# Edge weights made in PSUM in every layer, and one-hot matrices made tile by tile

## The chip, the cores and the metric

The kernel runs on one core of a Trainium2 chip. The metric is the time of one execution on the device in microseconds, as the median of three runs.

## The reference

A graph network of three layers over 6250 nodes and 100,000 edges, 256 features wide. Edges are sorted by destination, and the destinations are denser at low node numbers.

```python
ew = edge_attr @ edge_w + edge_b                      # [100000, 32] @ [32, 256]
rel_masks = [(edge_type == i) for i in range(3)]
inv_cnt = [1 / max(segment_sum(m, dst), 1) for m in rel_masks]
for l in range(3):
    residual = x
    msg = relu(x[src] * ew)
    out = 0
    for i in range(3):
        h = segment_sum(msg * rel_masks[i][:, None], dst) * inv_cnt[i][:, None]
        out = out + h @ weights[l, i]
    out = out + x @ roots[l] + biases[l]
    x = residual + relu(out)
return layernorm(x0 + x)                              # x0: the input x
```

The edge weights `ew` do not depend on the layer.

## The kernel before

Edges are taken in 782 tiles of 128, and two tiles make a pair; there are 391 pairs. A layer is one loop over steps `it`. Each step handles several pairs at different stages of one software pipeline, and the program's order within a step is each engine's order, since the schedule is written out by hand. `order` lists the pairs: from number 60 upward to the last, then from 59 down to 0. `pair(k)` is the pair that is k steps ahead.

For each pair of tiles:

- `gather` (L575, POOL's queue) fetches the source rows `x[src]` by two indirect DMAs, one for each tile, into `xs`, a tile with 16 buffers. It runs `AHEAD` = 8 steps ahead.
- `weigh` (L612, VectorE) multiplies `xs` by the edge weights, three steps ahead; `bound` (L615, ScalarE) applies the relu.
- `one_hot` (L619, VectorE) makes, for both tiles by one instruction, a matrix of 128 edges by 120 columns (three relations by 40 node places) that is one where the column equals the edge's number in `seg`.
- `reduce` (L629, TensorE) multiplies messages by one-hots, which sums the messages of the 40 nodes for each relation, into `h_p` in PSUM.
- `add` (L645, VectorE) adds `h_p` to the accumulator `acc` in SBUF, `LAG` steps later (1 in the first layer, 3 in the later ones).

In the first layer the edge weights are made as well. The raw attributes of eight tiles are loaded by one DMA (`load_attrs`), transposed on TensorE two pairs at a time (`turn`, L589, into `turn_p`), copied to SBUF by ScalarE (`keep_attrs`, L595, into `at`), multiplied by `edge_w` on TensorE (`make_ew`, L602, into `ew_p` in PSUM) and copied to SBUF by ScalarE (`keep_ew`, L609, into `ew_s`). Bias and product come in one matmul through a row of ones. From `ew_s`, four pairs at a time, 1 MB is stored to `ew_all` in DRAM (`store_ew`, SP's queue). The later layers load it back, 1 MB for four pairs (`load_ew`, L552, SP's queue).

Beside the edges run the nodes, 49 blocks of 128. `root_turn`, `root_turned`, `root_mul` and `root_keep` (L650 to L661) make x times `roots` and the bias. When the last edge of a block has been added, `node_mul` (L673, TensorE) multiplies the sums by `weights`, `node_end` (L700 to L707, VectorE) scales them, adds the root part, applies the relu and stores the block to `x_mid` in DRAM, and `clear` (L690, ScalarE) empties its place in `acc`. The steps at which blocks end come from `schedule`; they lie closer together as node numbers rise, because later nodes have fewer edges. The next layer's gathers read `x_mid`, so the first of them waits for its last store. In the last layer a layer norm follows each block (L710 to L721).

[...]

Of the kernel before, what the change touches and what calls it, by code (L numbers as in the profile page):

```python
# [442 lines left out]
def ordered_path(ctx, tc, x, edge_attr, weights, roots, biases, edge_w, edge_b, out, src_i, seg, place_i, consts):  # L443
# [13 lines left out]
    A1 = A + 1  # L457
    DC = D // P
    UP = P // 2
    AR = UP + A1  # L460
    WK = R * WIN
    AHEAD = 8
    order, _, moved, least, most = schedule(N, E, 1)
    reach = []
    for u, (lo, hi) in enumerate(zip(least, most)):
# [47 lines left out]
    groups = list(dict.fromkeys(u // 4 for u in order))  # L513

    def first_of(p, n):
        return p == 0 or order[p - 1] // n != order[p] // n

    def last_of(p, n):
        return p == U - 1 or order[p + 1] // n != order[p] // n
# [25 lines left out]
        nc.sync.dma_start(b_sb, biases[l:l + 1, :].to_broadcast([P, D]))  # L545
        return r_sb, b_sb

    def load_ew(l, g):
        ew = edge.tile([P, 4, 2, D], F32, name="ew_s", bufs=3)
        if l > 0:  # L550
            n = min(4, U - 4 * g)
            nc.sync.dma_start(ew[:, :n].rearrange("p k i d -> p (k i d)"), ew_all[g, :, :n * 2 * D])  # L552
        return ew

    def layer(l, r_sb, b_sb, ews, pools):
        h_pool = pools.enter_context(tc.tile_pool(name="h_p", bufs=2 if l == 0 else 5, space=PSUM))
        if l == 0:
            ew_pool = pools.enter_context(tc.tile_pool(name="ew_p", bufs=1, space=PSUM))
# [8 lines left out]
        xs, ew_ps, ats, ohs, h_ps, turns, o_ps, rs = {}, {}, {}, {}, {}, {}, {}, {}  # L567
        x0s, mvs, oh_bs, t_ss, places = {}, {}, {}, {}, []
        r_next, ews_next = (None, None), {}

        def gather(u):
            xs[u] = edge.tile([P, 2, D], F32, name="xs", bufs=16)
# [6 lines left out]
        def store_ew(g):  # L579
            n = min(4, U - 4 * g)  # L580
            nc.sync.dma_start(ew_all[g, :, :n * 2 * D], ews[g][:, :n].rearrange("p k i d -> p (k i d)"))

        def pairs_of(q):
            return range(min(2, U - 2 * q))
# [6 lines left out]

        def keep_attrs(q):
            n = len(pairs_of(q))
            ats[q] = edge.tile([AR, 2, P], F32, name="at", bufs=1)
            nc.scalar.activation(ats[q][:, :n], turns[q][:AR, :n, :], AF.Copy)  # L595

        def make_ew(q):

            ew_ps[q] = ew_pool.tile([P, 2, 2, D], F32, name="ew_p")
            for k in pairs_of(q):  # L600
                for i in range(2):
                    nc.tensor.matmul(ew_ps[q][:, i, k, :], ats[q][i * UP:i * UP + A1, k, :],  # L602
                                     ew_sb[i * UP:i * UP + A1, :], start=True, stop=True)

        def keep_ew(q):
            if q // 2 not in ews:
                ews[q // 2] = load_ew(0, q // 2)
            for k in pairs_of(q):
                nc.scalar.activation(ews[q // 2][:, q % 2 * 2 + k], ew_ps[q][:, :, k, :], AF.Copy)  # L609

        def weigh(u):
            nc.vector.tensor_mul(xs[u], ews[u // 4][:, u % 4], xs[u])  # L612

        def bound(u):
            nc.scalar.activation(xs[u], xs[u], AF.Relu)  # L615

        def one_hot(u):
            ohs[u] = edge.tile([P, 2, WK], F32, name="oh", bufs=6)
            nc.vector.tensor_tensor(ohs[u], iota_w[:, None, :].to_broadcast([P, 2, WK]),  # L619
                                    seg[:, 2 * u:2 * u + 2, None].to_broadcast([P, 2, WK]), op=ALU.is_equal)  # L620
# [120 lines left out]
        for it in range(-9, max(starts) + 6):  # L741
            def pair(k):
                return order[it + k] if 0 <= it + k < U else None
            if pair(AHEAD) is not None:
                gather(pair(AHEAD))
            if l == 0 and pair(9) is not None and first_of(it + 9, 4):
                load_attrs(pair(9) // 4)
            if l > 0 and pair(AHEAD) is not None and pair(AHEAD) // 4 not in ews:
                ews[pair(AHEAD) // 4] = load_ew(l, pair(AHEAD) // 4)
            if l == 0 and it >= -4 and (it + 4) % 20 == 0 and (it + 4) // 20 * 6 < NT - 1:  # L750
                load_x((it + 4) // 20 * 6)
            if it == 10:
                nc.sync.dma_start(w_sb, weights[l].rearrange("r (c p) e -> p (r c) e", p=P))
            if l == L - 1 and it + 2 in root_at:
                load_x0(root_at[it + 2])
            if l < L - 1 and it == U - 10:
                r_next = load_root(l + 1)
            if l < L - 1 and U <= it < U + 2:
                ews_next[groups[it - U]] = load_ew(l + 1, groups[it - U])
# [40 lines left out]
        return (*r_next, ews_next)  # L800

    with tc.manual_schedule():
        state = (*load_root(0), {})
# [4 lines left out]

WIN = 40
RING = 1024
ASIDE = RING + WIN
ROOTS = 16
PACK = 2048


def schedule(N, E, lag):

    P = 128
    U = -(-E // (2 * P))
    NT = -(-N // P)
    done = []
    for c in range(NT):
        edges = E * min(1.0, (P * (c + 1) / N) ** 0.5)
        done.append(U if c == NT - 1 else min(U, -(-int(edges) // (2 * P)) + 4))  # L830
    K = -(-done[0] // 4) * 4
# [12 lines left out]
    least = [node(2 * P * u - 1024) for u in range(U)]  # L844
    most = [node(2 * P * u + 1024) for u in range(U)]


    for p, u in enumerate(order, lag):
        if u >= K:
            assert all(p <= starts[c] or least[u] >= P * (c + 1) for c in range(2, NT))  # L850
            assert p <= moved or least[u] >= 2 * P
            assert all(p < starts[c] or least[u] >= P * c for c in range(8, NT, 8))
            for b in range(RING // P + 1, (most[u] + WIN - 1) // P + 1):
                assert (moved + 2 if b - RING // P == 1 else starts[b - RING // P] + 3) < p
        else:
            assert most[u] <= 2 * P and (p <= starts[1] or most[u] + WIN <= P)
    return order, starts, moved, least, most
# [149 lines left out]
```

## Time and profile before

| | |
|---|---|
| three runs | 3131.9, 3129.4, 3127.8 us; median 3129.4 |
| profiled execution | 3133.5 us, its span 3131.7 us |
| granted TensorE clock, mean | 0.855 |
| busy, share of the span | PE 78%, PE weight loads 67%, VectorE 64%, ScalarE 42%, POOL 75% |
| DMA | 668 MB, mean 213 GB/s; SP's and ScalarE's queues 32.2% of the engines, POOL's 31.6% |
| largest issues on SP | 194 loads of `ew_s` and 97 stores to `ew_all`, 1 MB each |
| gathers | 782 in the first layer, 1564 in the later two |

The busy share of an engine is the union of its instructions over the span. A group's line gives the program line, the engine, the operation, the tiles it writes and reads, shapes and count, then busy time and the mean of one instruction in nanoseconds, then the idle time in front of it and what ended that. A source line's answer gives the shortest, median and longest duration, and the starts of the first and last instruction. In the timeline each row begins with start and duration in microseconds. In a table by window the columns are length, PE, PE's weight loads, VectorE, ScalarE and POOL busy, then the clock, the DMA share and GB/s.

### The profile page before, as it was taken

How to read it: one execution, taken by the hardware profiler on the slowest of the kernel's cores; microseconds unless marked ns; L12 is line 12 of the kernel's file. 1: busy time of each engine (PE TensorE's matmuls, PEld its weight loads, DVE VectorE, ACT ScalarE, POOL GpSimd, SP SyncE). 2: the span in 40 equal slices, each digit the busy share in tenths (PEclk: the TensorE clock that was granted, in tenths of full speed). 3: DMA queues.
4: the chain of work that ended last, by engine and by line, in shares of the span. 5: the costliest groups of instructions: out<-in, count | busy, mean ns of one | idle time of the engine just before them, and what ended most of it. 6: DMA issues, size and time to landing. Idle time of an engine off the chain costs nothing.

```text
span 3131.7 us, 50860 instructions
## 1 busy us (share of the span) xinstructions
PE 2429.6 (78%) x14938; PEld 2108.6 (67%) x14938; DVE 2003.2 (64%) x4664; ACT 1302.0 (42%) x2524; POOL 2354.9 (75%) x3118
## 2 busy tenths in 40 slices
PE   4898999999998766677777777767677777877765
PEld 3777777778887666666666666656566666666665
DVE  4566666777776455566666666645566677777765
ACT  3666666666776422222333333222223333333332
POOL 7777777777777677777777777767777777777775
PEclk9899899999998778778888888766887888888886
DMA  4777776766776665656666666656666666666664
GB/s 135 233 233 231 222 241 213 228 216 217 230 231 213 217 218 199 213 200 218 205 217 205 221 221 217 206 184 223 211 208 223 220 217 209 224 228 216 218 216 138
DMA packets 295322, 668.14 MB, mean 213 GB/s; under 512 B 147224, under 2 KB 181996, under 8 KB 257788
## 3 DMA queue, kind: packets, MB, share of 16 engines
q1 hardware_dynamic: 175832, 350.27, 32.2%
q0 software_dynamic: 112608, 307.65, 31.6%
q10 hardware_dynamic: 6596, 6.87, 0.6%
q8 instruction: 124, 2.03, 0.3%
q14 instruction: 162, 1.33, 0.1%
HBM read 542.90 MB, written 121.70 MB: 212 GB/s over the span
## 4 chain that ended last, share of the span: by engine, by line
PE 31%; DMA 21%; issue 19%; POOL 17%; DVE 9%; ACT 2%; DVEq 1%; POOLq 0%; ACTq 0%
POOL xs L575 16%; PE h_p L629 15%; DMA xs<-x_mid,src_io 15%; PE o_p L673 7%; DMA xs<-in_x_dram,src_io 6%; PE ew_p L602 4%; DVE x_root L704 3%; DVE xs L612 2%; PE r_p L658 2%; DVE acc L645 2%; PE turn_p L589 1%; ACT ew_s L609 1%; POOL limits L926 1%; DVEq L645 1%; DVE oh L619 1%
## 5 line engine op out<-in xcount | busy, mean ns | idle before, releaser
L575 POOL DMA_INDIRECT xs<-x_mid,src_io x1564 | 1537.5, 983 | 509.0 <-issue 404.6
L629 PE MATMUL h_p<-oh,xs 128*128 128x120 f32 x9384 | 1451.6, 311 | 445.0 <-issue 177.8
L629 PEld LDWEIGHTS h_p<-oh,xs 128*128 128x128 f32 x9384 | 1364.3, 223 | 541.6 <-issue 309.4
L612 DVE TENSOR_TENSOR xs<-ew_s,xs 128x512 f32<-128x512 f32 x1173 | 808.0, 689 | 913.5 <-DMA xs<-x_mid,src_io 566.8
L615 ACT ACTIVATE xs<-xs 128x512 f32<-128x512 f32 x1173 | 739.5, 630 | 1484.9 <-DVE xs L612 1466.3
L575 POOL DMA_INDIRECT xs<-in_x_dram,src_io x782 | 789.6, 1010 | 247.1 <-issue 158.7
L645 DVE TENSOR_TENSOR acc<-h_p,acc 128x240 f32 (+1 forms) x1173 | 519.5, 443 | 147.0 <-PE h_p L629 74.7
L673 PE MATMUL o_p<-w_sb,acc 128*128 128x256 f32 (+1 forms) x1764 | 503.5, 428 | 89.2 <-DVE acc L645 52.1
L619 DVE TENSOR_TENSOR oh<-iota_w,seg_o 128x240 f32<-128x240 f32 x1173 | 467.0, 398 | 0.0
L673 PEld LDWEIGHTS o_p<-w_sb,acc 128*128 128x128 f32 (+1 forms) x1764 | 361.7, 216 | 152.4 <-DVE acc L645 57.6
L658 PE MATMUL r_p<-r_sb,t_s 128*128 128x256 f32 x588 | 216.3, 504 | 79.5 <-ACT t_s L654 78.8
L602 PE MATMUL ew_p<-ew_sb,at 33*128 33x256 f32 x1564 | 235.2, 421 | 10.9 <-ACT at L595 8.8
L609 ACT ACTIVATE ew_s<-ew_p 128x512 f32<-128x512 f32 x391 | 209.4, 587 | 41.5 <-PE ew_p L602 40.5
L704 DVE SCALAR_TENSOR_TENSOR x_root<-o_p,inv,x_root 128x256 f32<-128x256 f32 (+1 forms) x441 | 212.4, 482 | 20.9 <-PE o_p L673 8.6
L623 ACT ACTIVATE oh_b<-oh 128x240 bf16<-128x240 f32 x391 | 160.0, 409 | 117.9 <-DVE oh L619 111.0
L658 PEld LDWEIGHTS r_p<-r_sb,t_s 128*128 128x128 f32 x588 | 130.0, 245 | 111.3 <-ACT t_s L654 95.5
L602 PEld LDWEIGHTS ew_p<-ew_sb,at 33*128 33x128 f32 x1564 | 141.7, 195 | 44.8 <-ACT at L595 16.3
L690 ACT ACTIVATE acc<-zero_o 128x768 f32<-128x768 f32 (+1 forms) x150 | 141.0, 940 | 15.8 <-PE o_p L673 9.2
L629 PE MATMUL h_p<-oh_b,full_ones 128*128 128x120 bf16 x782 | 109.3, 223 | 0.0
L589 PE MATMUL turn_p<-ident_o,an 128*128 128x128 f32 x391 | 89.4, 312 | 7.9 <-DMA an<-in_edge_attr_dram 7.8
L589 PEld LDWEIGHTS turn_p<-ident_o,an 128*128 128x128 f32 x391 | 40.7, 145 | 77.1 <-issue 75.9
L650 PE MATMUL r_p<-ident_o,x_all 128*128 128x128 f32 x294 | 64.1, 303 | 30.9 <-DVE x_root L661 24.8
(84 smaller groups left out, 609.0 us busy)
## 6 DMA issues: line engine op xcount, KB each, us to landing
ew_s<-ew_all SPq DMA_DIRECT2D x194, 1024.0 KB
ew_all<-ew_s SPq DMA_DIRECT2D x97, 1024.0 KB
xs<-x_mid,src_io POOLq DMA_INDIRECT x1564
xs<-in_x_dram,src_io POOLq DMA_INDIRECT x782
an<-in_edge_attr_dram SPq DMA_DIRECT2D x97, 128.0 KB
x_mid<-x_all SPq DMA_DIRECT2D x96, 128.0 KB
x_all<-in_x_dram ACTq DMA_DIRECT2D x8, 768.0 KB
x<-in_x_dram SPq DMA_DIRECT2D x48, 128.0 KB
```

The lines of the kernel that those rows point to most:

```text
L575: nc.gpsimd.indirect_dma_start(out=xs[u][:, i, :], out_offset=None, in_=x_rows[:, :], in_offset=bass.IndirectOffsetOnAxis(ap=src_i[:, t:t ...
L589: nc.tensor.transpose(turns[q][:, k, :], ans[groups.index(q // 2) % 3][:, q % 2 * 2 + k].rearrange("p i a -> p (i a)"), ident)
L602: nc.tensor.matmul(ew_ps[q][:, i, k, :], ats[q][i * UP:i * UP + A1, k, :], ew_sb[i * UP:i * UP + A1, :], start=True, stop=True)
L609: nc.scalar.activation(ews[q // 2][:, q % 2 * 2 + k], ew_ps[q][:, :, k, :], AF.Copy)
L612: nc.vector.tensor_mul(xs[u], ews[u // 4][:, u % 4], xs[u])
L615: nc.scalar.activation(xs[u], xs[u], AF.Relu)
L619: nc.vector.tensor_tensor(ohs[u], iota_w[:, None, :].to_broadcast([P, 2, WK]), seg[:, 2 * u:2 * u + 2, None].to_broadcast([P, 2, WK]), op= ...
L629: nc.tensor.matmul(h_ps[u][:, d, :], xs[u][:, i, d * P:(d + 1) * P] if d < DC else full_ones, (ohs if d < DC else oh_bs)[u][:, i, :], star ...
L645: nc.vector.tensor_tensor(there, h_ps[u][:, :CH].rearrange("p c (r w) -> p c r w", r=R), there, op=ALU.add)
L658: nc.tensor.matmul(rs[c][:, 1, :], t_ss[c][:, d, :], r_sb[:, d, :], start=(d == 0), stop=(d == DC - 1))
L673: nc.tensor.matmul(o_p[:n, r, :], acc[:, d, r, slot:slot + n], w_sb[:, r * DC + d, :], start=(d == 0), stop=(d == DC - 1))
L704: nc.vector.scalar_tensor_tensor(root, o_p[:n, r, :], inv[:n, c, r:r + 1], root, op0=ALU.mult, op1=ALU.add)
```

## The change

The edge weights are no longer stored. The first layer keeps the transposed attributes instead, eight pairs (`GROUP`) in one tile `at` of 128 rows, and stores these to `at_all` in DRAM, 512 KB for eight pairs. The later layers load `at`, and every layer runs `make_ew` for two pairs at once. `weigh` takes the edge weights from `ew_p` in PSUM, so ScalarE's copy `keep_ew` and the tile `ew_s` are gone. A step that opens a new group of two pairs makes their weights first and weighs both pairs; the step after weighs none. `add` now stands ahead of `weigh` in a step. `h_p` has three buffers in the later layers, where `ew_p` takes two banks. `LAG` is 2 there, `AHEAD` is 9 in all, and the pairs turn around at 64.

`one_hot` uses two instructions, one for each tile, each with the tile's column of `seg` as a scalar for each partition.

```diff
-    AHEAD = 8
+    AHEAD = 9
...
-    ew_all = dram.tile([(U + 3) // 4, P, 8 * D], F32, name="ew_all")
+    at_all = dram.tile([(U + GROUP - 1) // GROUP, P, GROUP * P], F32, name="at_all")
...
-    def load_ew(l, g):
-        ew = edge.tile([P, 4, 2, D], F32, name="ew_s", bufs=3)
+    def pairs_in(g):
+        return min(GROUP, U - GROUP * g)
+
+    def load_at(l, g):
+        at = edge.tile([P, GROUP, P], F32, name="at", bufs=3)
         if l > 0:
...
+            nc.sync.dma_start(at[:, :pairs_in(g)].rearrange("p k e -> p (k e)"), at_all[g, :, :pairs_in(g) * P])
+        return at
...
-        h_pool = pools.enter_context(tc.tile_pool(name="h_p", bufs=2 if l == 0 else 5, space=PSUM))
+        h_pool = pools.enter_context(tc.tile_pool(name="h_p", bufs=2 if l == 0 else 3, space=PSUM))
+        ew_pool = pools.enter_context(tc.tile_pool(name="ew_p", bufs=1, space=PSUM))
...
-        LAG = 1 if l == 0 else 3
+        LAG = 1 if l == 0 else 2
...
         def keep_attrs(q):
             n = len(pairs_of(q))
-            ats[q] = edge.tile([AR, 2, P], F32, name="at", bufs=1)
-            nc.scalar.activation(ats[q][:, :n], turns[q][:AR, :n, :], AF.Copy)
+            g = 2 * q // GROUP
+            if g not in ats:
+                ats[g] = load_at(0, g)
+            nc.scalar.activation(ats[g][:, 2 * q % GROUP:2 * q % GROUP + n], turns[q][:, :n, :], AF.Copy)
...
-        def keep_ew(q):
-            if q // 2 not in ews:
-                ews[q // 2] = load_ew(0, q // 2)
-            for k in pairs_of(q):
-                nc.scalar.activation(ews[q // 2][:, q % 2 * 2 + k], ew_ps[q][:, :, k, :], AF.Copy)
-
         def weigh(u):
-            nc.vector.tensor_mul(xs[u], ews[u // 4][:, u % 4], xs[u])
+            nc.vector.tensor_mul(xs[u], ew_ps[u // 2][:, :, u % 2, :], xs[u])
...
         def one_hot(u):
             ohs[u] = edge.tile([P, 2, WK], F32, name="oh", bufs=6)
-            nc.vector.tensor_tensor(ohs[u], iota_w[:, None, :].to_broadcast([P, 2, WK]),
-                                    seg[:, 2 * u:2 * u + 2, None].to_broadcast([P, 2, WK]), op=ALU.is_equal)
+            for i in range(2):
+                nc.vector.tensor_scalar(ohs[u][:, i, :], iota_w, seg[:, 2 * u + i:2 * u + i + 1], None,
+                                        op0=ALU.is_equal)
...
+            two = [order[p] for p in range(it + 3, min(it + 5, U)) if order[p] // 2 == pair(3) // 2] if (
+                pair(3) is not None and first_of(it + 3, 2)) else []
+            if two:
+                make_ew(two[0] // 2)
             if pair(0) is not None:
                 reduce(pair(0))
-            if pair(3) is not None:
-                weigh(pair(3))
-                bound(pair(3))
             if pair(-LAG) is not None:
                 add(pair(-LAG))
+            for u in two:
+                weigh(u)
+                bound(u)
             if l == 0:
 
-                for k, work in ((4, keep_ew), (5, make_ew), (6, keep_attrs), (7, turn)):
+                for k, work in ((5, keep_attrs), (6, turn)):
                     if pair(k) is not None and first_of(it + k, 2):
                         work(pair(k) // 2)
-                if pair(3) is not None and last_of(it + 3, 4):
-                    store_ew(pair(3) // 4)
+                if pair(3) is not None and last_of(it + 3, GROUP):
+                    store_at(pair(3) // GROUP)
...
-    K = -(-done[0] // 4) * 4
+    K = -(-done[0] // GROUP) * GROUP
```

More of the change, by code (lines that the diff above doesn't have):

```diff
@@ L459, in ordered_path @@
     UP = P // 2
-    AR = UP + A1
     WK = R * WIN
-    AHEAD = 8
+    AHEAD = 9
     order, _, moved, least, most = schedule(N, E, 1)
@@ L513, in ordered_path @@
     groups = list(dict.fromkeys(u // 4 for u in order))
+    at_groups = list(dict.fromkeys(u // GROUP for u in order))
     def first_of(p, n):
@@ L546, in load_root, with layer @@
         return r_sb, b_sb
-    def load_ew(l, g):
-        ew = edge.tile([P, 4, 2, D], F32, name="ew_s", bufs=3)
+    def pairs_in(g):
+        return min(GROUP, U - GROUP * g)
+    def load_at(l, g):
+        at = edge.tile([P, GROUP, P], F32, name="at", bufs=3)
         if l > 0:
[L551 to L555, printed above, removed]
-        h_pool = pools.enter_context(tc.tile_pool(name="h_p", bufs=2 if l == 0 else 5, space=PSUM))
+            nc.sync.dma_start(at[:, :pairs_in(g)].rearrange("p k e -> p (k e)"), at_all[g, :, :pairs_in(g) * P])
+        return at
+    def layer(l, r_sb, b_sb, ats, pools):
+        h_pool = pools.enter_context(tc.tile_pool(name="h_p", bufs=2 if l == 0 else 3, space=PSUM))
+        ew_pool = pools.enter_context(tc.tile_pool(name="ew_p", bufs=1, space=PSUM))
         if l == 0:
-            ew_pool = pools.enter_context(tc.tile_pool(name="ew_p", bufs=1, space=PSUM))
             t_pool = pools.enter_context(tc.tile_pool(name="turn_p", bufs=1, space=PSUM))
-        LAG = 1 if l == 0 else 3
+        LAG = 1 if l == 0 else 2
         starts = schedule(N, E, LAG)[1]
@@ L566, in layer @@
         CH = DC + 1 if l == 0 else DC
-        xs, ew_ps, ats, ohs, h_ps, turns, o_ps, rs = {}, {}, {}, {}, {}, {}, {}, {}
+        xs, ew_ps, ohs, h_ps, turns, o_ps, rs = {}, {}, {}, {}, {}, {}, {}
         x0s, mvs, oh_bs, t_ss, places = {}, {}, {}, {}, []
-        r_next, ews_next = (None, None), {}
+        r_next, ats_next = (None, None), {}
         def gather(u):
@@ L577, in gather, with store_at @@
                     in_offset=bass.IndirectOffsetOnAxis(ap=src_i[:, t:t + 1], axis=0))
-        def store_ew(g):
-            n = min(4, U - 4 * g)
-            nc.sync.dma_start(ew_all[g, :, :n * 2 * D], ews[g][:, :n].rearrange("p k i d -> p (k i d)"))
+        def store_at(g):
+            nc.sync.dma_start(at_all[g, :, :pairs_in(g) * P], ats[g][:, :pairs_in(g)].rearrange("p k e -> p (k e)"))
         def pairs_of(q):
@@ L601, in make_ew @@
                 for i in range(2):
-                    nc.tensor.matmul(ew_ps[q][:, i, k, :], ats[q][i * UP:i * UP + A1, k, :],
+                    nc.tensor.matmul(ew_ps[q][:, i, k, :],
+                                     ats[2 * q // GROUP][i * UP:i * UP + A1, (2 * q + k) % GROUP, :],
                                      ew_sb[i * UP:i * UP + A1, :], start=True, stop=True)
-        def keep_ew(q):
-            if q // 2 not in ews:
-                ews[q // 2] = load_ew(0, q // 2)
-            for k in pairs_of(q):
-                nc.scalar.activation(ews[q // 2][:, q % 2 * 2 + k], ew_ps[q][:, :, k, :], AF.Copy)
         def weigh(u):
-            nc.vector.tensor_mul(xs[u], ews[u // 4][:, u % 4], xs[u])
+            nc.vector.tensor_mul(xs[u], ew_ps[u // 2][:, :, u % 2, :], xs[u])
         def bound(u):
@@ L747, in layer @@
                 load_attrs(pair(9) // 4)
-            if l > 0 and pair(AHEAD) is not None and pair(AHEAD) // 4 not in ews:
-                ews[pair(AHEAD) // 4] = load_ew(l, pair(AHEAD) // 4)
+            if l > 0 and pair(AHEAD) is not None and pair(AHEAD) // GROUP not in ats:
+                ats[pair(AHEAD) // GROUP] = load_at(l, pair(AHEAD) // GROUP)
             if l == 0 and it >= -4 and (it + 4) % 20 == 0 and (it + 4) // 20 * 6 < NT - 1:
@@ L758, in layer @@
             if l < L - 1 and U <= it < U + 2:
-                ews_next[groups[it - U]] = load_ew(l + 1, groups[it - U])
+                ats_next[at_groups[it - U]] = load_at(l + 1, at_groups[it - U])
+            two = [order[p] for p in range(it + 3, min(it + 5, U)) if order[p] // 2 == pair(3) // 2] if (
+                pair(3) is not None and first_of(it + 3, 2)) else []
+            if two:
+                make_ew(two[0] // 2)
             if pair(0) is not None:
                 reduce(pair(0))
-            if pair(3) is not None:
-                weigh(pair(3))
-                bound(pair(3))
             if pair(-LAG) is not None:
                 add(pair(-LAG))
+            for u in two:
+                weigh(u)
+                bound(u)
             if l == 0:
-                for k, work in ((4, keep_ew), (5, make_ew), (6, keep_attrs), (7, turn)):
+                for k, work in ((5, keep_attrs), (6, turn)):
                     if pair(k) is not None and first_of(it + k, 2):
                         work(pair(k) // 2)
-                if pair(3) is not None and last_of(it + 3, 4):
-                    store_ew(pair(3) // 4)
+                if pair(3) is not None and last_of(it + 3, GROUP):
+                    store_at(pair(3) // GROUP)
             if it in root_at:
@@ L799, in layer @@
                 one_hot(pair(3))
-        return (*r_next, ews_next)
+        return (*r_next, ats_next)
     with tc.manual_schedule():
@@ L814 @@
 ROOTS = 16
+GROUP = 8
 PACK = 2048
```

## The prediction

> **What bounds the kernel now.** I read the engine table first: PE has the largest busy share, which need not make it the bound. Then the costliest groups, then the gathers' own line.
>
> ```profile
> PE 2429.6 (78%) x14938; PEld 2108.6 (67%) x14938; DVE 2003.2 (64%) x4664; ACT 1302.0 (42%) x2524; POOL 2354.9 (75%) x3118
> ...
> L575 POOL DMA_INDIRECT xs<-x_mid,src_io x1564 | 1537.5, 983 | 509.0 <-issue 404.6
> L612 DVE TENSOR_TENSOR xs<-ew_s,xs 128x512 f32<-128x512 f32 x1173 | 808.0, 689 | 913.5 <-DMA xs<-x_mid,src_io 566.8
> L575 POOL DMA_INDIRECT xs<-in_x_dram,src_io x782 | 789.6, 1010 | 247.1 <-issue 158.7
> L619 DVE TENSOR_TENSOR oh<-iota_w,seg_o 128x240 f32<-128x240 f32 x1173 | 467.0, 398 | 0.0
> ```
> ```profile
> L575 POOL DMA_INDIRECT xs<-x_mid,src_io x1564: 942/946/1456, 1082.1 to 3111.4; - x196
> L575 POOL DMA_INDIRECT xs<-in_x_dram,src_io x782: 942/946/1627, 38.3 to 1064.9; - x196
> ...
>   DMA x_mid<-x_all: 32.8, 2
> ```
>
> POOL issues 2346 gathers back to back from 38.3 to 3112.3 us. In 3074 us it is busy 1537.5 + 789.6 = 2327.1; the other 747 are a constant 0.30 us between two gathers (2343 x 0.305 = 714) and two waits at the layer changes (32.8). It never waits for a buffer, so in steady state nothing else sets the pace. The span is 38.3 start + 2346 x 0.946 = 2219 + lengthened gathers 108 + 747 between + 19.4 tail = 3131.7.
>
> The 108 us: the median gather takes 946 ns, the means are 983 and 1010, so 1564 x 0.037 + 782 x 0.064 = 108. The timeline shows where they come from.
>
> ```profile
> 1608.44 0.94 POOL L575 DMA_INDIRECT xs<-x_mid,src_io  x1 [0.30 <-DMA xs<-x_mid,src_io]
> 1609.57 0.69 DVE L612 TENSOR_TENSOR xs<-ew_s,xs 128x512 f32<-128x512 f32 x1 [1.61 <-DMA xs<-x_mid,src_io]
> 1609.69 1.39 POOL L575 DMA_INDIRECT xs<-x_mid,src_io  x1 [0.30 <-issue]
> ...
> 1611.05 0.68 DVE L612 TENSOR_TENSOR xs<-ew_s,xs 128x512 f32<-128x512 f32 x1
> 1611.38 1.17 POOL L575 DMA_INDIRECT xs<-x_mid,src_io  x1 [0.30 <-issue]
> ...
> 1613.54 1.51 DVE L704 SCALAR_TENSOR_TENSOR x_root<-o_p,inv,x_root 128x256 f32<-128x256 f32 x3
> ...
> 1614.42 0.95 POOL L575 DMA_INDIRECT xs<-x_mid,src_io  x1 [0.30 <-issue]
> ```
>
> A gather that starts while `weigh` (L612, both inputs in SBUF) runs lasts 0.946 plus what is left of the `weigh`, less 0.127: 1609.69 starts with 0.57 left and takes 1.39. One that starts under L704, whose first input is PSUM, takes 0.95. I sorted all gathers of the trace by the DVE instruction running at their start: under L612 480, lengthened by 82.4 us in all; under L619 (one-hots, both inputs SBUF) 349 by 22.6; under other instructions with two SBUF inputs 3; under none (873), or one with a PSUM input (L645 355, L704 161, L661 41), zero.
>
> **The change, part by part.** The sum is made against the profiled execution (span 3131.7, time 3133.5; the median of the three runs is 4.1 below).
>
> `weigh` from PSUM: its second input leaves SBUF, so the 82.4 go. Its own time stays 0.69: L661 (PSUM and SBUF) has 414 ns, L663 (both SBUF) 415 at the same 128x256.
>
> One-hots: the tensor_tensor of 398 ns becomes two tensor_scalars of 120 elements with a scalar column. The 22.6 of the old form go. The nearest row is L719.
>
> ```profile
> L719 DVE TENSOR_SCALAR x_all<-x_all,mv x49: 411/423/572, 2244.8 to 3125.4; 128x256 f32<-128x256 f32 x48, 106x256 f32<-106x256 f32 x1
> ```
> Taking off 136 elements at 1.07 ns (the slope from L619 to L612) gives 0.27 us; at half that slope 0.34. I take 0.27. Successive DVE instructions start about 0.08 before the former's end, so a pair's one-hots cost 0.38 of DVE instead of 0.32: 70 us more over 1173 pairs, up to 235 at 0.34. DVE is 64% busy and trails POOL, so this alone is free.
>
> [...] Fourteen gathers start under L719: none is lengthened. But L719 itself grows: eighteen that start with 0.3 to 0.4 us of a gather left average 505 ns. [...] I take 5, keep 0 to 25.
>
> Edge weights on PE: layers 2 and 3 gain 391 x 4 matmuls with their weight loads. In layer 1's timeline eight records (one group of two pairs) go from 700.58 to the next PE group at 701.65: 1.07, so 0.535 per pair, 209 us per layer. Those layers keep PE busy 66 to 78% of each 200 us window at a granted clock of 0.72 to 0.89, so there is room. In layer 1 nothing is added, but PE has no room.
>
> ```profile
> 660.00:860.00 200.00, 192.62 (x1430) 161.69 (x1429) 146.49 (x335) 139.15 (x295) 153.68 (x153) 1.00 0.70 222
> 1660.00:1860.00 200.00, 155.45 (x909) 138.36 (x908) 133.83 (x314) 65.09 (x109) 152.56 (x156) 0.89 0.64 212
> ```
> First column after the length is PE: 192.6 of 200 at full clock in layer 1, 155.5 in layer 2. In layer 1's stretch of close node blocks (17 in 70 pairs by the schedule) PE needs, from starts in the timeline, 70 x (0.99 reduce + 0.535 weights + 0.14 turns) + 17 x 2.96 node products + 12 x 1.09 root products = 180 us; POOL without lengthening passes those pairs in 70 x 2.50 = 175. So half of layer 1 (460 to 960) cannot speed up: 25 of its 50 us stay.
>
> New waits there: `ew_p` is one buffer, freed by DVE's second `weigh` instead of ACT's copy, and that `weigh` waits for its gather. Behind it on DVE stand the one-hots and the next `add`; `reduce` on PE waits for both (`h_p` has two buffers in layer 1, three later instead of five). With 16 gather buffers POOL can run about 10 pairs, 25 us, beyond today's lag (reduce starts 11 to 18 us after the gather in layer 1), which absorbs most. `add` now stands ahead of the `weigh`s in the step, so it no longer waits for a gather with them; the order's turning point moves from pair 60 to 64, which shifts node blocks by 4 steps and costs nothing. No row shows the loop; its bounds are 0 and, if every pair of layer 1 paid 0.2 us beyond POOL's pace, 80. I take 10.
>
> Layer changes: the drain now includes weights on PE; LAG falls by one. I add 2 each, 4.
>
> Removed: 194 loads and 97 stores of 1 MB on SP's queue (some 307 of 668 MB) and 391 ACT copies (209 us). No gather waits for them; ACT is at 42%. Cost nothing, bring nothing, except that landings (L612 waits 566.8 us for them) may come sooner. Stores and loads of `at`, half a MB per eight pairs, ride the same queue, nine pairs ahead. The gather's distance 8 to 9 only reaches deeper into buffers that never ran out.
>
> Sum: -105 + 5 + 25 + 10 + 4 = -61. Span 3071, time 3072.5; less 4.1 against the median: **3068 us**, 2% faster.
>
> **Rivals.**
> (1) Nothing else binds: -105 + 5, about 3029. For it: POOL never waits today, and 25 us of lag can hide layer 1's stretch. Against it: PE at 96% there.
> (2) The loop PE, DVE, PE over one `ew_p` costs some 60 more in layer 1 and the dense end of layer 3: 3110 to 3135. Against it: per pair of groups PE's weights and two `weigh`s take 1.07 + 1.38 of 5.0 us.
> (3) Slower: DVE becomes the bound because the one-hots wait for the gather. Per pair in layer 1 DVE needs `weigh` 0.61 + `add` 0.45 + node work 0.33 plus two one-hots; it reaches POOL's 2.50 when one costs 0.55, in the dense stretch (0.26 more node work) at 0.42. From about 0.5 the loss exceeds 100. At 0.6, layer 1's average is 2.59, the dense stretches 2.85: some 90 us slower than before, 3220. For it: L719's longest is 572. Against it: only starts late in a gather grew, by 0.1 on average.
> (4) The lengthening does not go, because some other SBUF read replaces it: 3131 plus 25 to 40 of waits, 3165. Against it: 557 gathers under PSUM-fed instructions, not one lengthened.
>
> **How the numbers follow.** The sum above 0.52 (3040 to 3100), rival 1 0.17, rival 2 0.16 (three quarters still faster), rival 3 0.10, rival 4 0.05. Range 3028 to 3130: it leaves out rivals 3 and 4 and a little at each end. About 0.2% (6 us) can be told from no change. Faster 0.80, same 0.04, slower 0.16. The sum's own range stands in brackets above.
>
> **What would show it.** Right: L575's means fall to 946 to 955 and no gather is lengthened under the weigh line; POOL's waits for "PE h_p" appear in layer 1 alone, 10 to 50 us; layers 2 and 3 shorten by 25 to 30 each, layer 1 by 10 to 20; PE in layers 2 and 3 rises to 85 to 95%. Wrong: one-hots of 0.4 us or more; gathers still near 990; POOL waiting for PE in layers 2 and 3 for more than 30 us; DVE over 85%.

## The result, and the profile after

The changed kernel takes 3096.0 us (median of four runs, 3093.1 to 3105.5) against 3128.7 us before: a ratio of 0.9893, 95% interval 0.9879 to 0.9908. That is clear of the noise, though little. The direction and the mechanism were forecast; the gain is 33 us where 61 were. The profiled execution took 3096.8 us, its span is 3094.9, 36.8 shorter than before.

From the page after: the engines, and the groups that answer to those shown of before (busy time, mean ns; idle time in front).

```profile
PE 2707.7 (87%) x18066; PEld 2214.5 (72%) x18066; DVE 2073.9 (67%) x5837; ACT 1110.3 (36%) x2133; POOL 2260.6 (73%) x3118
...
L576 POOL DMA_INDIRECT xs<-x_mid,src_io x1564 | 1489.6, 952 | 533.6 <-issue 363.5
...
L609 DVE TENSOR_TENSOR xs<-ew_p,xs 128x512 f32<-128x512 f32 x1173 | 766.3, 685 | 811.4 <-PE ew_p L604 549.4
L576 POOL DMA_INDIRECT xs<-in_x_dram,src_io x782 | 743.1, 950 | 278.6 <-issue 154.1
...
L617 DVE TENSOR_SCALAR oh<-iota_w,seg_o 128x120 f32<-128x120 f32 x2346 | 578.4, 297 | 0.0
```

The gathers' means fell from 983 and 1010 ns to 952 and 950. Sorted as before by the VectorE instruction running at their start, 499 gathers begin under `weigh` and none is lengthened; 372 under a one-hot, by 6.3 us in all. All lengthening together is 13.4 us, where it was 107.8. So 94.4 us went. They did not all arrive.

The gathers' own line, with the start of the first and last of each kind, and two of the waits listed under it:

```profile
L576 POOL DMA_INDIRECT xs<-x_mid,src_io x1564: 940/946/1569, 1066.9 to 3073.2; - x196
...
L576 POOL DMA_INDIRECT xs<-in_x_dram,src_io x782: 940/946/1486, 38.3 to 1050.0; - x196
...
  DMA x<-in_x_dram: 18.9, 1
  DMA x_mid<-x_all: 15.9, 1
```

From these and the trace's gathers I take each layer from its first gather to the end of its last, and what the gaps between gathers hold beyond the usual 0.30 us:

| | before | after | stalls of POOL after |
|---|---|---|---|
| layer 1 | 1027.6 | 1012.7 | 32, between 650 and 1000 us |
| layer 2 | 1005.5 | 981.8 | 0.1 |
| layer 3 | 1008.2 | 1006.6 | 23, between 2750 and 3000 us |
| the two layer changes | 16.2, 16.6 | 15.9, 18.9 | |
| tail | 19.4 | 20.7 | |

Within the layers POOL stalled for 0.3 us before. -94.4 + 32 + 0.1 + 23 + 3.4 (changes and tail) is -36, the span's -36.8. Layer 2 keeps its whole gain; layer 3 keeps nearly none, as it gives it back in its last third. There `reduce` starts up to 51 us after its gather (10 at the layer's beginning); in layer 2 it averages 9 to 14 over each tenth of the layer. At an estimated 40 us (16 pairs at 2.5) the gather buffers are used up and POOL waits.

Windows in layers 1, 2 and 3; the columns are length, PE, PE's weight loads, VectorE, ScalarE, POOL, granted clock, DMA share and GB/s.

```profile
660.00:860.00 200.00, 184.21 (x1322) 149.23 (x1323) 138.50 (x378) 95.15 (x202) 132.76 (x141) 1.00 0.49 138
1660.00:1860.00 200.00, 181.69 (x1210) 150.40 (x1206) 140.74 (x394) 64.63 (x109) 151.55 (x160) 0.97 0.47 140
2660.00:2860.00 200.00, 172.14 (x1053) 140.81 (x1050) 141.30 (x412) 60.20 (x110) 140.39 (x148) 0.90 0.44 134
```

In layer 2 TensorE is busy for 91% of the time and POOL is not held up. In layer 3's dense end POOL is slower and TensorE is *less* busy than in layer 2: 172 of 200. So TensorE is not simply full there; it waits. For what, the timeline shows:

```profile
2753.92 1.51 DVE L702 SCALAR_TENSOR_TENSOR x_root<-o_p,inv,x_root 128x256 f32<-128x256 f32 x3
...
2755.47 0.43 DVE L703 SCALAR_TENSOR_TENSOR x_all<-x_root,x_all 128x256 f32<-128x256 f32 x1
...
2755.93 0.43 DVE L708 BATCH_NORM_STATS2 stats<-x_all 128x6 f32<-128x256 f32 x1
2756.39 0.18 DVE L710 BATCH_NORM_AGGREGATE mv<-stats 128x2 f32<-128x6 f32 x1
...
2756.60 0.29 ACT L711 ACTIVATE mv<-mv,eps 128x1 f32<-128x1 f32 x1 [3.30 <-DVE mv L710]
...
2756.90 0.39 DVE L643 TENSOR_TENSOR acc<-h_p,acc 128x240 f32 x1
...
2757.39 1.12 PE L627 MATMUL h_p<-oh,xs 128*128 128x120 f32 x8 [1.75 <-ACT mv L711]
```

TensorE stands for 1.75 us ahead of a `reduce`. The row names the square root on ScalarE (L711) as releaser, but that ended at 2756.89. The `add`, which gives an `h_p` buffer back, ended at 2757.29, and TensorE starts 0.10 later. I measured all 36 waits over 0.5 us ahead of a `reduce` in layer 3: in 35 of them (62 us) TensorE starts 55 or about 101 ns after the end of an `add`, and anything from 387 to 3537 ns after a square root; the other is the last of the kernel. The releaser is the `add`, and on VectorE it stands behind 3.3 us of node work, in layer 3 with the layer norm's statistics in it, and two one-hots.

### The profile page after: what moved, and what is told of

It is laid out like the page before. It is cut to its first block, busy times and chain, and to the rows that moved or that the text cites. A ratio compares the mean times of both kernels' runs of the same rounds, so it can differ in the third digit from the quotient of the medians.

```text
span 3094.9 us, 57973 instructions
## 1 busy us (share of the span) xinstructions
PE 2707.7 (87%) x18066; PEld 2214.5 (72%) x18066; DVE 2073.9 (67%) x5837; ACT 1110.3 (36%) x2133; POOL 2260.6 (73%) x3118
## 5 line engine op out<-in xcount | busy, mean ns | idle before, releaser
L576 POOL DMA_INDIRECT xs<-x_mid,src_io x1564 | 1489.6, 952 | 533.6 <-issue 363.5
L627 PEld LDWEIGHTS h_p<-oh,xs 128*128 128x128 f32 x9384 | 1230.1, 205 | 352.3 <-issue 197.0
L627 PE MATMUL h_p<-oh,xs 128*128 128x120 f32 x9384 | 1366.7, 297 | 119.3 <-ACT mv L711 45.1
L612 ACT ACTIVATE xs<-xs 128x512 f32<-128x512 f32 x1173 | 724.8, 630 | 1689.6 <-DVE xs L609 1641.6
L609 DVE TENSOR_TENSOR xs<-ew_p,xs 128x512 f32<-128x512 f32 x1173 | 766.3, 685 | 811.4 <-PE ew_p L604 549.4
L576 POOL DMA_INDIRECT xs<-in_x_dram,src_io x782 | 743.1, 950 | 278.6 <-issue 154.1
L604 PE MATMUL ew_p<-ew_sb,at 33*128 33x256 f32 x4692 | 703.7, 420 | 95.6 <-DVE xs L609 74.1
L643 DVE TENSOR_TENSOR acc<-h_p,acc 128x240 f32 (+1 forms) x1173 | 516.3, 440 | 142.6 <-PE o_p L671 64.1
L604 PEld LDWEIGHTS ew_p<-ew_sb,at 33*128 33x128 f32 x4692 | 429.6, 195 | 243.3 <-issue 159.0
L617 DVE TENSOR_SCALAR oh<-iota_w,seg_o 128x120 f32<-128x120 f32 x2346 | 578.4, 297 | 0.0
L671 PE MATMUL o_p<-w_sb,acc 128*128 128x256 f32 (+1 forms) x1764 | 462.3, 401 | 28.1 <-DVE acc L643 15.0
L671 PEld LDWEIGHTS o_p<-w_sb,acc 128*128 128x128 f32 (+1 forms) x1764 | 338.0, 202 | 74.8 <-DVE acc L643 17.2
L627 PEld LDWEIGHTS <-full_ones 128*128 128x128 bf16 x782 | 81.2, 104 | 2.3
L597 ACT ACTIVATE at<-turn_p 128x256 f32<-128x256 f32 x196 | 71.5, 365 | 0.7 <-PE turn_p L589 0.7
```

The source lines that it names most:

```text
L576: nc.gpsimd.indirect_dma_start(out=xs[u][:, i, :], out_offset=None, in_=x_rows[:, :], in_offset=bass.IndirectOffsetOnAxis(ap=src_i[:, t:t ...
L604: nc.tensor.matmul(ew_ps[q][:, i, k, :], ats[2 * q // GROUP][i * UP:i * UP + A1, (2 * q + k) % GROUP, :], ew_sb[i * UP:i * UP + A1, :], st ...
L609: nc.vector.tensor_mul(xs[u], ew_ps[u // 2][:, :, u % 2, :], xs[u])
L617: nc.vector.tensor_scalar(ohs[u][:, i, :], iota_w, seg[:, 2 * u + i:2 * u + i + 1], None, op0=ALU.is_equal)
L627: nc.tensor.matmul(h_ps[u][:, d, :], xs[u][:, i, d * P:(d + 1) * P] if d < DC else full_ones, (ohs if d < DC else oh_bs)[u][:, i, :], star ...
L643: nc.vector.tensor_tensor(there, h_ps[u][:, :CH].rearrange("p c (r w) -> p c r w", r=R), there, op=ALU.add)
```

## The experiments

The twelve runs fell on different chips. On one the kernel before takes 3124 us, much as above; on three others 3684, 3642 and 3642 us, and there the engines stand still for microseconds at a time (shown below). Times are compared within one chip only. What a gather takes is the same on all, a median of 946 to 949 ns.

**The second SBUF input or the traffic?** The first four runs, on the chip of 3684 us. `weigh_sbuf` keeps the new flow of attributes and lets ScalarE copy the weights from PSUM, so `weigh` has two SBUF inputs again.

```diff
+        def copy_ew(u):
+            ew_cs[u] = edge.tile([P, 2, D], F32, name="ew_c", bufs=4)
+            nc.scalar.activation(ew_cs[u], ew_ps[u // 2][:, :, u % 2, :], AF.Copy)
...
-            nc.vector.tensor_mul(xs[u], ew_ps[u // 2][:, :, u % 2, :], xs[u])
+            nc.vector.tensor_mul(xs[u], ew_cs[u], xs[u])
```

> The changed kernel, but ScalarE copies each pair's weights from PSUM to SBUF and the weigh takes both inputs from SBUF; no DRAM traffic is added (it stays at 438 MB). If a DVE instruction with two SBUF inputs holds up a gather that starts under it: about 480 gathers lengthened again by some 80 us in all, means of the gathers 975 to 990 ns instead of 951, time near 3096 + 80 less 10 to 30 of stalls that a slower stream hides: 3140 to 3170 us. If the 668 MB of transfers before were what lengthened them: means stay at 950, time 3090 to 3110 us.

Measured: 3880.3 us, 1.053 (1.051 to 1.055) of the kernel before. Its groups:

```profile
L576 POOL DMA_INDIRECT xs<-x_mid,src_io x1564 | 1563.6, 1000 | 942.1 <-issue 594.6
...
L576 POOL DMA_INDIRECT xs<-in_x_dram,src_io x782 | 772.1, 987 | 532.1 <-issue 242.3
```

With DMA traffic as in the changed kernel (438 MB) the gathers are long again: 116 us of lengthening, 109 of them in 462 gathers that start under `weigh`. So the second SBUF input does it, and the 230 MB that the change saves do not.

`onehot_old`, the changed kernel with the one comparison of two SBUF operands in place of two scalar ones:

```diff
-            for i in range(2):
-                nc.vector.tensor_scalar(ohs[u][:, i, :], iota_w, seg[:, 2 * u + i:2 * u + i + 1], None,
-                                        op0=ALU.is_equal)
+            nc.vector.tensor_tensor(ohs[u], iota_w[:, None, :].to_broadcast([P, 2, WK]),
+                                    seg[:, 2 * u:2 * u + 2, None].to_broadcast([P, 2, WK]), op=ALU.is_equal)
```

> The changed kernel with the old one-hot, one tensor_tensor for a pair of tiles. If two SBUF inputs are the cause: gathers that start under it lengthened by some 20 to 25 us in all instead of 6, DVE 0.06 to 0.1 us less per pair; time 3096 plus 5 to 15 us: 3098 to 3112. If the transfers were the cause: no gather lengthened, and the shorter DVE work makes it 3080 to 3095 us.

> The changed kernel with the one-hot matrices of a pair of tiles made again by one comparison of two SBUF operands instead of two with a scalar for each edge. Theory A (a gather that starts while an operation with two SBUF operands runs on VectorE lasts longer, one that starts under the scalar form nearly does not): gathers starting under the one-hot are lengthened by 60 to 90 ns on average, 20 to 30 us in all, as in the same kernel's profile on the slow chip (24.7 us), against 6 us; the time rises by 5 to 20 us over the unchanged kernel, ratio 0.989 to 0.994; part of the lengthening is absorbed where POOL stalls anyway in layers 1 and 3. Theory B (the form of the one-hot makes no difference to POOL; the gain came from the weights in PSUM alone): lengthening under the one-hot stays under 10 us, ratio 0.985 to 0.989.

Measured: 1.034 (1.032 to 1.036) and, on a chip of 3642 us, 1.037 (1.033 to 1.040). Both are chips on which the times decide nothing. The lengthening does: 24.7 and 24.1 us under the old one-hot (291 and 296 gathers), against 6.3 under the scalar form. The first theory's size, 20 to 30.

`before_onehot` is the reverse: the kernel before with nothing but the scalar one-hots.

> The kernel before with the new one-hot alone (two tensor_scalars for a pair). If two SBUF inputs are the cause: the 22.6 us under the one-hot fall to about 6, the 82 us under the weigh stay or grow a little, total lengthening 85 to 95 instead of 108; time 3129 less 10 to 20: 3109 to 3120 us. If the transfers were the cause: lengthening stays at 108, time 3125 to 3135 us.

Measured: 3686.9 against 3684.2 us, 1.0002 (0.9989 to 1.0016).

```profile
L575 POOL DMA_INDIRECT xs<-x_mid,src_io x1564 | 1557.7, 996 | 830.9 <-issue 618.4
L575 POOL DMA_INDIRECT xs<-in_x_dram,src_io x782 | 776.9, 993 | 469.2 <-issue 248.6
```

Lengthening 115 us, where 85 to 95 were expected: nothing gained. Under `weigh` it is 80 us, and 29 still under the one-hots, by up to 721 ns, though the same form costs 6 us in the changed kernel. Of these 29 us 24.7 lie in 37 gathers, the only ones that grew by more than 0.1 us, and in each of them a `weigh` begins 96 to 169 ns after the gather's start: a `weigh` that begins just behind the start holds the gather up as well. Part by part, in these traces: the scalar one-hots bring nothing while `weigh` still reads SBUF twice, and the weights in PSUM alone leave 24 us under the old one-hots.

`xs23`: seven more gather buffers.

```diff
-            xs[u] = edge.tile([P, 2, D], F32, name="xs", bufs=16)
+            xs[u] = edge.tile([P, 2, D], F32, name="xs", bufs=23)
```

> The changed kernel with 23 instead of 16 gather buffers. If the 32 us of POOL stalls in layer 1 and 23 in layer 3 arise because the work behind falls back in the stretch of close node blocks only for a while, seven pairs (17.5 us) of further distance take that much out of each: stalls 15 and 6, time 3062 to 3072 us. If the work behind is slower than POOL up to the layer's end, the layer changes grow by what the stalls lose: 3090 to 3098 us.

Measured: 3871.5 us, 1.050 (1.047 to 1.052) on the chip of 3684; POOL stalls 845 us there, layer changes included, over all layers and in pieces of some 2 us. The gathers are as in the changed kernel (951 and 949 ns). That is not a matter of buffers, and the run says nothing on the question.

**Where layers 1 and 3 lose.** Four runs on a chip where the kernel before takes 3124.1 us.

> The changed kernel again, unchanged, as the measure for the three beside it. In the first comparison it took 0.989 of the time of the kernel before; in the runs since, on a chip on which the kernel before took 3684 us instead of 3129, the three kernels derived from it took 1.034 to 1.053 of it. Theory A (that chip holds the engines up by an amount that grows with the instructions, and the changed kernel has 57,973 against 50,860 instructions): on such a chip the unchanged kernel too stands at 1.03 to 1.06, and on a chip where the kernel before takes 3129 us it is again at 0.989. Theory B (the edits of those three kernels made them slow): it stands at 0.98 to 1.00 on either chip.

Measured: 3087.0 us, 0.9875 (0.9850 to 0.9899). The first result again. What the unchanged kernel does on the slower chips was not run.

> The changed kernel with 23 gather buffers instead of 16, so that the reduction may fall 13 us (7 x 1.9) further behind before a gather waits. Theory A (layers 1 and 3 lose 32 and 23 us because the loop of weights, weighing and sums falls behind by up to 50 us, and the gathers wait when the 16 buffers are used up): with 7 more buffers up to 13 us are absorbed in layer 1 and, as the layer's end is dense, up to 13 us less POOL stall in layer 3, but the backlog must then be worked off after the last gather, so the layer change grows by what is saved: the time falls by 0 to 15 us against the unchanged kernel. Theory B (POOL waits for something other than free buffers): POOL stalls and time within 3 us of the unchanged kernel.

Measured: 3075.4 us, 0.9841 (0.9819 to 0.9862); its four runs end at 3077.7 where the unchanged kernel's begin at 3082.9. From the gathers' own line:

```profile
L576 POOL DMA_INDIRECT xs<-in_x_dram,src_io x782: 940/946/1324, 38.3 to 1031.3; - x196
...
  DMA x_mid<-x_all: 32.6, 1
```

Layer 1's gathers end 15 us sooner (993.9 instead of 1009.0 us from the first) and then the wait at the layer change is 17 us longer, 32.6 instead of 15.8: `reduce` is 37 us behind in layer 1's last tenth, where it was 19, and layer 2's gathers need its rows. Layer 3 keeps its 18.6 us: the tail behind its last gather is 21.4 us, where the unchanged kernel has 22.2, so this backlog is worked off under the last gathers. The stalls are for buffers, as the first theory had it; that layer 1's part comes back at the layer change, too. Of the versions that leave nothing out this is the fastest that was run.

`weigh_first` puts the two weighings ahead of the `add` in each step again.

```diff
+            for u in two:
+                weigh(u)
+                bound(u)
             if pair(-LAG) is not None:
                 add(pair(-LAG))
-            for u in two:
-                weigh(u)
-                bound(u)
```

> The changed kernel with the two weighings issued ahead of the addition into the accumulator in each step, as they stood before the change. Theory A (the loop falls behind because the weighing stands behind an addition that waits about 2 us for node products still reading the accumulator, so the weights' PSUM banks are freed late): the add's wait no longer holds the weighing, POOL stalls in layers 1 and 3 fall from 32 and 23 us to under 20 in all, and the time falls by 20 to 40 us. Theory B (the loop falls behind because TensorE has no room in the dense parts, whatever the order on VectorE): stalls within 10 us of the unchanged kernel's, time within 10 us; a later add may hold TensorE (h_p) and cost up to 20 us.

Measured: 3219.3 us, 1.0289 (1.0256 to 1.0322), 132 us slower than the unchanged kernel. Neither theory. The waits of the changed kernel, then of this one (total, times, longest):

```profile
DVE xs L609 <- PE ew_p L604: 549.4, 346, 6.1
...
PE h_p L627 <- DVE acc L643: 39.7, 45, 2.9
```
```profile
DVE xs L609 <- PE ew_p L604: 943.7, 420, 7.0
...
PE h_p L627 <- DVE acc L643: 183.1, 196, 4.3
```

In 420 of the 588 steps that make weights `weigh` waits for them, for TensorE makes them in the same step. With the `add` behind it, the `add` waits too, and TensorE's next `reduce` waits for the `add`'s `h_p` buffer. POOL stalls 70, 7 and 89 us in the three layers. The move of `add` ahead of `weigh`, one line of the diff, is what lets the new flow pay at all.

`no_norm` leaves out layer 3's layer norm.

> The changed kernel without the layer normalisation of layer 3 (bn_stats, bn_aggr, square root, reciprocal, subtract and multiply left out; the rows are stored as they are). TensorE's work is the same. Theory A (layer 3 falls behind, where layer 2 with the same TensorE work does not, because its node work on VectorE and ScalarE is longer and weighing and sums wait behind it): layer 3's POOL stall goes from 23 us to under 5, and the time falls by 20 to 30 us, about 5 of it from the tail after the last gather. Theory B (TensorE alone is too full in the dense end of layer 3): the stall stays at 15 us or more and the time falls by 10 us or less.

Measured: 3068.3 us, 0.9815 (0.9794 to 0.9836), 18.8 us below the unchanged kernel. Layer 3's stall is gone (no gap beyond the usual one), its gathers take 982.5 us, as layer 2's do, where the unchanged kernel beside it took 1003.6. The window that answers to the third above:

```profile
2660.00:2860.00 200.00, 183.84 (x1211) 151.86 (x1211) 142.58 (x406) 64.40 (x108) 151.26 (x161) 0.97 0.48 146
```

TensorE does the same work and is busier, POOL runs at full pace, VectorE is as busy as before (142.6), since the steps come faster. TensorE's waits ended by an `add` in layer 3 go from 62.5 us to 33.4, what layer 2 has (30.4). The first theory holds, a little under its 20 to 30 us: the layer norm's node work is what makes layer 3 fall behind.

**Which queue of the two?** `sqrt_late` moves only ScalarE's square root to the next step and the norm one further; `stats_late` moves VectorE's statistics along with it.

```diff
-            nc.scalar.activation(mv[:n, 2:3], mv[:n, 1:2], AF.Sqrt, bias=eps[:n])
+        def root_var(c):
+            n = min(P, N - c * P)
+            nc.scalar.activation(mvs[c][:n, 2:3], mvs[c][:n, 1:2], AF.Sqrt, bias=eps[:n])
...
             if it - 4 in node_at and l == L - 1:
+                root_var(node_at[it - 4])
+            if it - 5 in node_at and l == L - 1:
-                norm(node_at[it - 4])
+                norm(node_at[it - 5])
```
```diff
                 return
+
+        def var(c):
+            n = min(P, N - c * P)
             stats = edge.tile([P, nc.vector.BN_STATS_DIM], F32, name="stats")
...
             if it - 4 in node_at and l == L - 1:
+                var(node_at[it - 4])
+            if it - 5 in node_at and l == L - 1:
-                norm(node_at[it - 4])
+                norm(node_at[it - 5])
```

> The changed kernel with the square root of layer 3's layer norm issued one step later on ScalarE (behind the next step's relu) and the norm two steps behind the node products' end instead of one. Nothing is left out. Leaving out the layer norm took layer 3's POOL stall from 23 us to none and 19 us from the time; the trace names the wait of TensorE's sums as one for the square root (98 us in all), and ScalarE waits 3.3 us for bn_aggr ahead of it. Theory A (ScalarE's queue is what holds up the sums: the relu, or the clearing, behind a square root that waits for VectorE): layer 3's stall falls from 23 us to under 8 and the time by 12 to 20 us against the unchanged kernel's ratio of 0.9875, to 0.982 to 0.984. Theory B (VectorE's queue does: the addition that frees an h_p buffer stands behind 3.3 us of node work, and the square root merely ends at the same moment): the stall stays at 17 to 25 us and the ratio within 0.002 of 0.9875.

> The changed kernel with bn_stats, bn_aggr and the square root of layer 3's layer norm issued one step later (behind the next step's addition and weighing on VectorE), the norm in the step after that. Nothing is left out, VectorE's and TensorE's work is the same. Theory B (the addition that frees one of three h_p buffers waits behind one unbroken 3.3 us stretch of node work on VectorE; broken in two pieces of 2.6 and 0.6 us it holds TensorE for less): layer 3's stall falls from 23 us to 5 to 15, ratio 0.983 to 0.986. Theory A (ScalarE's queue): the square root still waits for bn_aggr in its own step, but now only some 0.7 us, so the stall falls too, to under 8. Theory C (it is the sum of VectorE's work in the dense end of layer 3, not its order): the stall stays at 17 to 25 us, ratio within 0.002 of 0.9875.

> The kernel of the run before once more: bn_stats, bn_aggr and the square root of layer 3's layer norm one step later, the norm two steps behind the node products' end; nothing is left out. In the changed kernel's trace every one of 35 long waits of TensorE's sums in layer 3 ends 55 or 102 ns after an addition that frees an h_p buffer, and between 387 and 3537 ns after a square root, so VectorE's queue is the one to shorten. On a chip where the kernel before takes about 3125 us: Theory B (the addition behind one unbroken stretch of node work) layer 3's stall of POOL falls from 23 us to 5 to 15, ratio 0.982 to 0.986 against 0.9875 of the unchanged kernel; Theory C (the sum of VectorE's work, not its order) 17 to 25 us, ratio within 0.002 of 0.9875. On a chip where the kernel before takes over 3600 us: nothing can be told of this, ratio 1.03 to 1.05 as for the three kernels like it.

Measured, on two chips of 3642 us: 1.045 (1.0417 to 1.0484), 1.039 (1.0369 to 1.0412) and 1.038 (1.0345 to 1.0416). The times can't decide it: POOL stalls some 730 to 760 us here, layer changes included, and the four runs of `sqrt_late` alone lie between 3753 and 3814 us. TensorE's waits over 0.5 us that end with an `add` can still be counted. Layer 2, which has no layer norm, is the measure within each trace:

| us | layer 2 | layer 3 |
|---|---|---|
| the changed kernel | 31.4 | 61.9 |
| square root moved | 40.6 | 73.7 |
| statistics moved | 51.4, 46.5 | 46.0, 49.4 |
| without the norm | 31.5 | 33.4 |

With the square root moved layer 3 still waits 33 us longer than layer 2, as in the changed kernel (30); with the statistics moved what it has beyond layer 2 is gone. (The first and last rows are from the faster chips.) Together with the 55 and 101 ns above, that speaks for VectorE's queue; what breaking it up is worth in time stays open.

What the slower chips do is seen in this stretch of `sqrt_late`:

```profile
1609.45 0.41 DVE L643 TENSOR_TENSOR acc<-h_p,acc 128x240 f32 x1
1609.48 0.73 PEld L604 LDWEIGHTS ew_p<-ew_sb,at 33*128 33x128 f32 x8
1609.48 1.13 PE L604 MATMUL ew_p<-ew_sb,at 33*128 33x256 f32 x8
...
1618.05 1.29 DVE L609 TENSOR_TENSOR xs<-ew_p,xs 128x512 f32<-128x512 f32 x2 [8.19 <-remote]
...
1618.77 1.23 ACT L612 ACTIVATE xs<-xs 128x512 f32<-128x512 f32 x2 [9.64 <-DVE xs L609]
```

By the rows the weights are made by 1610.6, and VectorE begins to use them at 1618.05, 8.19 us after its last work; the row gives no instruction that released it. ScalarE and, at 1619.5, TensorE follow it. But the trace also holds the updates of the semaphores, each with its time. The one that this `weigh` waits for is TensorE's, and it was updated at 1618.02, 0.02 us before the `weigh` starts. So VectorE does wait for TensorE, whose update comes 7.4 us after the weights' rows end (the profile models the ends of matmuls). It is so throughout: in the changed kernel's trace 2632 of TensorE's 2635 recorded updates come within 0.1 us of the end of a matmul's row. In `sqrt_late` 1147 of 2377 do, and 412 come over 1.5 us after it, while VectorE's and ScalarE's come within 0.1 us there too (3050 of 3052 and 1402 of 1404). Of VectorE's 455 waits over 1 us in `sqrt_late` 392 end within 0.04 us of an update by TensorE.

The kernel before has such stops as well: in `before_onehot` POOL stalls 577 us, layer changes included, and 619 of TensorE's 2109 updates are over 1.5 us late. Seven runs of kernels that differ from the changed one in one place took 1.034 to 1.053 of the kernel before on these chips, so the change, which gives TensorE more to do, probably loses there. Why TensorE's updates are late on them was not found; part of the updates is also missing from these traces (`sqrt_late` has 3052 of VectorE's 4452).

## Why the prediction was right, and where not

**Lengthening: right.** Predicted to go: the 82.4 us under `weigh`, all of it, and the 22.6 under the one-hots with 5 coming back. Measured: 0 left under `weigh`, 6.3 under the scalar one-hots. Some 7 remain under other instructions with SBUF inputs (L703 3.9, L661 2.1, L682 1.2), where 3 were. Net 94 instead of 100. No run shows the term of 5 us that the prediction takes back; the trace after has 6.3 in its place: 372 gathers under a `tensor_scalar` grew by 17 ns on average, 117 at most. The row of L719, where none of fourteen gathers grew, came close.

**One-hots and `weigh`: nearly.** `weigh` from PSUM takes 685 ns (690 said). A one-hot's median is 274 ns (270), its mean 297, since the ones that start with 0.3 to 0.5 us of a gather left take some 400. Rival 3 needed one-hots of 0.42 us or more; VectorE is at 67%.

**Layer 1: the number right, its reason not shown.** Predicted 25 + 10 us kept back, measured 32; 15 us shorter, within 10 to 20. But the 25 were for a TensorE without room, and in the window from 660 us it is busy 184.2 of 200 us at full clock, less than the 192.6 of before, while POOL issues 141 gathers instead of 153. So it isn't simply full there either. How the 32 divide between its work and the new waits was not measured.

**Layer changes: right**, 2.1 and another 1.3 in the tail, for 4.

**Layer 3: the step that failed.** The prediction gave the loop of `ew_p`, VectorE and `reduce` 10 us, saw POOL's waits "in layer 1 alone", and let the 25 us that POOL can run ahead absorb most of the rest. In layer 3 it lost 23. That is rival 2's place, at less than its price. The step read TensorE's room in the later layers from its busy share (155 of 200) and did not ask how evenly that room lies. The edge weights took most of it (TensorE is busy 181.7 of 200 in layer 2, 91%), and in layer 3 each node block then holds TensorE for some 1.8 us behind one `add`, about every 15 us between 2640 and 2780 us. As an estimate, 0.91 + 1.8/15 is 1.03 of POOL's pace, where layer 2's waits of 1.0 us each make 0.98. So the backlog grows, to 51 us, past what 16 buffers hold. `no_norm` puts a price on it: 21 us of gather time in layer 3. The waits themselves are not new. With five `h_p` buffers the kernel before has 50 over 0.5 us in layer 3, 91 us in all, and POOL did not stall; TensorE had the room:

```profile
2660.00:2860.00 200.00, 154.58 (x889) 135.28 (x888) 149.61 (x377) 66.76 (x123) 152.77 (x156) 0.87 0.67 223
```

Whether five buffers would still help the changed kernel was not tried.

**What was to show it.** Gather means, `weigh` and layer 1 came as written, layer 2 nearly (24 us shorter, 25 to 30 said), layer 3 did not (1.6). Nor did POOL's waits carry the name "PE h_p" (48.0 us in 155 waits, hardly more than the usual 0.30 each): the longest entry with a releaser is "ACT xs L612", 93.0 us in 167.

## What to carry to other kernels

When an indirect gather on POOL sets the pace, sort its durations by the VectorE instruction that runs at their start; one SBUF operand moved to PSUM freed 82 us here, and cutting the traffic was no part of it. An engine that gets work in "free" room must have that room at the places where others wait for it: look at the densest stretch of each stage, and at what the program puts on the same engine ahead of the instruction that frees a buffer (in layer 3, 3.3 us of node work and two one-hots). Give a backlog more buffers only where the stage's end can absorb it; in layer 1 of `xs23_again` the wait at the layer change grew by 17 us at once.

## What was not expected of the hardware

In this case TensorE's granted clock rose with its load: 0.855 to 0.928 over the kernel, 0.89 to 0.97 in layer 2's window, where it is busy 182 of 200 us instead of 155, while layer 3's window, with its pauses, has 0.90 and goes to 0.97 once the layer norm is left out. The share of busy time alone does not set it: `weigh_first`, busy for 84%, was granted 0.944, and in layer 2's window 0.99 with 175.4 of 200 us busy. The mean product of `reduce` went from 311 to 297 ns, that of the node blocks (L671) from 428 to 401; their busy time fell by 85 and 41 us. So TensorE's busy time rose by 278 us, though the rows of the weights alone grew by 468 (235.2 to 703.7; the prediction's 2 x 209 count from start to start).

A named releaser can be one that merely ended last but one: all waits on "ACT mv L711" (45 us) were waits for an `add`. A constant distance from the true releaser's end, here 100 to 102 ns, gave it away. And where a row names no releaser there can be one all the same, as the semaphores' updates showed on the slower chips.

The kernel before took 3124, 3642 and 3684 us on different chips. In the traces from them instruction times outside TensorE are nearly equal (gathers 946 to 949 ns by the median, `weigh` 684 to 689 in the mean).
